# Row fetches of 128 indices, one column group per compare, and 26 dense blocks in the first layer of a three-layer graph network

## The chip, the cores and the metric

The kernel runs on one core of one Trainium2 chip. The metric is the device time of one execution in microseconds, the median of three runs. The chip's engines have short names in the profile: PE (the matrix engine, with PEld for its weight loads), DVE (VectorE), ACT (ScalarE), POOL (GpSimd) and SP (SyncE, which here only issues DMAs). Each runs its own list of instructions in order. GpSimd issues the indirect DMAs that fetch table rows by index.

## The reference, cut to what matters

```python
# x: 6250 x 256 float32; src, dst: 100000 int32, sorted by dst
def gcn(h, W, b):
    h = h @ W
    return segment_sum(h[src] * norm_edge[:, None], dst, n) + b
# src, dst are extended by one loop per node, (i, i)
# deg[d] = number of edges into d (with the loop); norm_edge = deg[src]**-0.5 * deg[dst]**-0.5
h = x                                              # 256
for W, b in ((W1, b1), (W2, b2), (W3, b3)):        # 256 -> 512 -> 512 -> 256
    h = relu(gcn(h, W, b))
out = layernorm(x + h, eps=1e-5)
```

A layer sums, for every node, the rows of the nodes that point to it (16 edges a node on average) and multiplies by a weight matrix. The factors deg**-0.5 belong to the source and the target, so a table holds rows already scaled by the source's factor, and the target's factor comes after the sum.

## The kernel before, in words

**Two ways of summing.** The 6250 nodes are 50 blocks (`NB`) of 125 (`Q`). The sum over incoming edges is made for a whole block at a time, in one of two ways. A *dense* block takes the 125 x 6250 matrix of edge counts (`kept`, stored in bytes) and multiplies it on PE by all rows of the table, held in SBUF as `parts`, a rounded half and a remainder: 50 matmuls at L1467, one for each block of sources, with five blocks' counts converted at a time into a `piece` (L1347). A *gathered* block fetches rows from the table in DRAM with indirect DMAs (L1383) into a ring of row buffers (`rows`). For each block there are 14 *rounds* (`ROUNDS`): round r fetches the source of the r-th edge of each of the 125 nodes, so DVE can add the 125 rows straight to the block's running sum (L1440, `total`). A node with fewer than 14 edges has the index N there, the table's row of zeros. Edges past the 14th are fetched in 128-row lists, three a block (`beyond`), one for two blocks (`pair`) and one for ten (`shared`). ACT and DVE cut these rows into two halves (L1434, L1437), and PE multiplies them by a one-hot matrix (L1399) into the node's place. The index lists are `round_src` (125 partitions), `over_src` and `rest` (128 partitions).

**Which blocks, in which layer.** `layer` (L1267) runs a layer. In layer 1 blocks 0 to 23 (`FEW`) are dense and 26 are gathered: 458 fetches. In layer 2 the first 12 blocks are dense, by `teams` (L1127, matmuls at L1197, three blocks at a time), from the counts kept in layer 1; 38 are gathered: 669 fetches. In layer 3 blocks 0 to 31 (`MANY`) are dense and 18 gathered: 317 fetches. Rows are 256 floats wide in layers 1 and 3 and 512 in layer 2. Layer 2 has 10 row buffers, layer 3 has 19.

**The order of the work.** It is written out by hand. The loop of `layer` takes one fetch at a time (a *chunk*, `now`): it issues fetch `chunk`, adds the round of a few chunks ago (`ADDED`, 3, 5 and 3), cuts and multiplies older lists (`SPLIT`), advances the generators that run beside it (`go_fixed`, `go`), and issues as many dense matmuls as the chunk's number allows:

```python
until = min(len(dense) * NB, begun + int((chunk + 1 - first) * NB / spacing)) if dense else 0
...
if chunk >= total - 1:
    until = len(dense) * NB
```

`spacing` is the number of chunks for each dense block, 16 in layer 1; a dense block also has to wait until its counts are there, and after the last chunk all the remaining matmuls are issued. Each fetch waits until the ring's buffer has been freed by the sum that read it.

**What else runs in layer 1.** The *finder* makes the index lists: `found_rounds` (L576) writes `round_src` for two blocks, with small matmuls into a PSUM bank and a row of small DVE instructions, four of them at L601; `found_beyond` (L615) writes `over_src`. `all_found` runs the first a few pairs ahead of the second. The bank they use (`spot[0]`) is the second half of the PSUM tile whose first half, `near_cols`, holds a copy of `keys`, the numbers of the columns. `counts` (L999) makes the count matrices: for each window of 128 edges it compares edge numbers with column numbers and so has a one-hot matrix of 128 x 125 (`hot_lo`) and one of 128 x 250 (`hot_key`) in bfloat16; PE multiplies the two (L1092), ACT copies the result into the block's counts (L1054), and SP stores them. The compares are made for five windows (`WIDE`) at a time by `compared` (L1018), in three instructions of five, three and two windows, 625, 750 and 500 elements a partition. In layer 1 the counts of blocks 0 to 27 (`FEW + EXTRA`) are made; those of the other four blocks that layer 3 needs are made in layer 2, by `counts_alone`, beside the fetches. `keys` and `slots`, from which `numbers` is cut, lie in SBUF in bfloat16; the copy `near_cols` is float32.

**Between layers.** A block's sum goes through `after1`, `after2` or `after3`: scaling, transposing, matmul with the weights, and the store of the next table. A layer's fetches can begin only when the table before it is complete, so each layer ends in a tail without fetches. `teams` begins its sums when the dense blocks of layer 1 are finished (`while finished < FEW`), and `home` brings back the rows that `teams` had no room for.

Of the kernel before, what the change touches and what calls it, by code (L numbers as in the profile page):

```python
# [13 lines left out]
I32 = mybir.dt.int32  # L14
# [8 lines left out]
P = 128  # L23
# [3 lines left out]
Q = 125  # L27
# [19 lines left out]
FEW = 24  # L47
EXTRA = 4
# [11 lines left out]
ADDS = (False, False, False)  # L60
TURNS = 4
# [338 lines left out]
def sorted_path(ctx: ExitStack, tc: tile.TileContext, x, edges, starts, found, wts, biases, room, late, out):  # L400
# [35 lines left out]
    round_src = const.tile([Q, NE, ROUNDS], I32, name="round_src")  # L436
# [70 lines left out]
    def finder_numbers(spare):  # L507
# [44 lines left out]
        nc.vector.memset(over_lo[:, :, BEYOND], float(P - 1))  # L552
        yield
# [22 lines left out]
    def found_rounds(e):  # L576
# [34 lines left out]
        nc.vector.tensor_single_scalar(round_src[:, e:e + 2], real, float(N), op=ALU.add)  # L611
# [130 lines left out]
    with tc.tile_pool(name="sdeg1", bufs=1) as dp1, tc.tile_pool(name="sdeg", bufs=2) as dp, \  # L742
# [139 lines left out]
        with tc.manual_schedule():  # L882
# [101 lines left out]
    totals = totals_of(one, "sfirst_totals", C, 3) + [first_rows.pop() for _ in range(2 * TURNS - 3)] if ADDS[0] else totals_of(one, "sfirst_totals", C, 3)  # L984
# [14 lines left out]
    def counts(blocks, places, rush=0, at_once=False):  # L999
# [18 lines left out]
        def compared(out, numbers):  # L1018
            shape = list(out.shape)
            nc.vector.tensor_tensor(out, near_cols[:, :shape[2]].unsqueeze(1).to_broadcast(shape),  # L1020
                                    numbers.unsqueeze(2).to_broadcast(shape), op=ALU.is_equal)
# [245 lines left out]
    def layer(i, width, first_b, dense, after, rows, first=0, spacing=None, extras=(), filler=None):  # L1267
# [3 lines left out]
        adds, most_of_acc = ADDS[i], 2 if i == 1 else 3  # L1271
# [7 lines left out]
        together = TURNS if adds else 1  # L1279
        for n in range(0, len(gathered), together):  # L1280
            bs = gathered[n:n + together]
            items += [("round", b, r) for r in range(ROUNDS) for b in bs]
            for b in bs:
                if b == first_b or b % GRP == 0:
                    items.append(("shared", b, b // GRP))
                if b % 2 == 0:
                    items.append(("pair", b, 0))
                items += [("beyond", b, j) for j in range(BEYOND)]
# [65 lines left out]
        def gather(c):  # L1354
# [3 lines left out]
            if kind == "round":  # L1358
                while e not in rounds_ready:
                    next(finding)  # L1360
                if j == 0:
                    sums[b] = totals[b % len(totals)][:Q]
                    by_rows(nc.sync, sums[b], tables[i][b * Q:(b + 1) * Q, :])
                if adds:
                    nc.gpsimd.indirect_dma_start(out=sums[b], out_offset=None, in_=tables[i],
                                                 in_offset=bass.IndirectOffsetOnAxis(ap=round_src[:, e, j:j + 1], axis=0),
                                                 compute_op=ALU.add)
                    return
# [21 lines left out]
        def kind_at(c):  # L1390
            return items[c][0] if 0 <= c < total else None
# [32 lines left out]
        with tc.manual_schedule():  # L1424
            for chunk in range(total + lag):
# [12 lines left out]
                if kind_at(chunk - ADDED[i]) == "round" and not adds:  # L1438
# [258 lines left out]
    layer(0, C, FEW, few, after1, first_rows, 16, 16.0,  # L1697
# [28 lines left out]
    totals = totals_of(ctx, "slate_totals", C, 2 * TURNS if ADDS[2] else 3)  # L1726
# [184 lines left out]
```

## Time and profile before

| | |
|---|---|
| median of three runs | 2670.28 us (2648.01 to 2673.69) |
| profiled execution, its own time | 2664.05 us |
| its span in the trace | 2662.3 us |
| busy: PE, DVE, POOL, ACT | 1923.2 (72%), 1781.3 (67%), 1804.2 (68%), 1099.5 us (41%) |
| moved by DMA | 452.97 MB, 170 GB/s over the span |
| of it in GpSimd's queue (row fetches) | 274.22 MB, 217984 packets |
| row fetches | 1148 by `round_src`, 287 by `over_src`, 9 by `rest` |
| chain that ended last | DMA 49%, DVE 22%, PE 10%, issue 10% |

In the profile, a group of instructions has its line, engine, operation, output and inputs by the program's names, the shapes as partitions x elements, the number of instructions, the busy time and the mean of one in ns, and then the idle time of the engine ahead of them with what ended it (`<-DVE total L1440` means that a DVE instruction of L1440 released it). A line of the time line has the start in us, the duration, and in brackets the idle time before it. A stretch has, for each engine, busy us and the number of instructions, then the granted clock of the matrix engine (1.00 is full), the busy share of the 16 DMA engines and what they moved. A fetch's DMA view shows a window in 40 slices, with the busy share of the DMA engines in tenths in each.

### The profile page before, as it was taken

To read this page: it belongs to the slowest core of one execution; us is meant where nothing else is said; L and a number is where in the kernel's file an instruction comes from. 1 tells how busy PE (TensorE), PEld (TensorE's weight loads), DVE (VectorE), ACT (ScalarE), POOL (GpSimd) and SP (SyncE) were. 2 spreads that over 40 slices of the span, in tenths; PEclk is the share of its full clock that TensorE was granted. 3 is DMA by queue.
4 is the path that set the end of the run, shared out by engine and by line. 5 is a ranking of instruction groups with operands and counts; after the bars stand their busy time and mean duration, and the time that the engine had idled before them with its cause. 6 is when DMAs were issued, how large, how long until landed. Compare 5 with 4: busy or idle time off the path is not lost.

```text
span 2662.3 us, 29214 instructions
## 1 busy us (share of the span) xinstructions
PE 1923.2 (72%) x7865; PEld 1410.1 (53%) x7865; DVE 1781.3 (67%) x3890; ACT 1099.5 (41%) x2136; POOL 1804.2 (68%) x1487
## 2 busy tenths in 40 slices
PE   3367777777788765778767777777674579898885
PEld 2245555555565443556545655555453357676663
DVE  5789889897898835656566565556665536666656
ACT  1455556555676632333334333332331234343432
POOL 2365656665677746777777677667778858787776
PEclk9988888898999776788887888788887779999998
DMA  6434434343455689999999999999997747776764
GB/s 141 121 92 113 116 91 132 110 110 110 116 145 142 187 193 206 204 207 230 224 211 222 221 223 217 207 224 216 211 216 196 190 127 169 169 174 168 172 169 116
DMA packets 331628, 452.97 MB, mean 170 GB/s; under 512 B 169007, under 2 KB 219174, under 8 KB 331453
## 3 DMA queue, kind: packets, MB, share of 16 engines
q0 software_dynamic: 217984, 274.22, 46.4%
q1 hardware_dynamic: 97629, 164.94, 25.3%
q10 hardware_dynamic: 15840, 11.86, 1.9%
q8 instruction: 63, 1.03, 0.2%
q14 instruction: 112, 0.92, 0.1%
HBM read 392.59 MB, written 57.00 MB: 169 GB/s over the span
## 4 chain that ended last, share of the span: by engine, by line
DMA 49%; DVE 22%; PE 10%; issue 10%; POOL 5%; ACT 2%; SPq 1%; ACTq 0%; DVEq 0%; POOLq 0%
DMA room<-tab,round_src 36%; DMA room<-tab,over_src 9%; DVE room L1020 6%; DVE total L1440 5%; POOL room L1383 5%; PE sacc L1467 1%; DMA room<-in_x 1%; DVE halves L1437 1%; DMA total<-tab 1%; PE mat_ps L1467 1%; DMA room<-tab,rest 1%; DVE st L1521 1%; ACT halves L1434 1%; DVE emask L601 1%; PE smm L1467 1%
## 5 line engine op out<-in xcount | busy, mean ns | idle before, releaser
L1383 POOL DMA_INDIRECT room<-tab,round_src x1148 | 1481.2, 1290 | 626.9 <-DVE total L1440 238.6
L1440 DVE TENSOR_TENSOR total<-total,room 125x256 f32<-125x256 f32 (+1 forms) x1148 | 625.8, 545 | 584.8 <-DMA room<-tab,round_src 565.5
L1383 POOL DMA_INDIRECT room<-tab,over_src x287 | 291.6, 1016 | 144.4 <-issue 41.4
L1347 ACT CAST piece<-room 125x625 fp32r<-125x625 uint8 x457 | 321.4, 719 | 123.7 <-PE win_ps L1467 30.2
L1434 ACT CAST halves<-room 128x256 fp32r<-128x256 f32 (+1 forms) x296 | 149.3, 508 | 528.1 <-DMA room<-tab,over_src 480.0
L1020 DVE TENSOR_TENSOR room<-near_cols,slots 128x625 bf16<-128x625 f32 (+2 forms) x420 | 325.2, 803 | 52.6 <-PE near_cols L625 26.3
L1197 PE MATMUL sacc<-parts 125*125 125x512 f32 x400 | 183.1, 510 | 188.2 <-DVE parts L1161 167.2
L1399 PE MATMUL sacc<-halves,shot 128*125 128x512 f32 x525 | 206.1, 492 | 108.3 <-ACT halves L1434 63.0
L1467 PE MATMUL win_ps<-parts,piece 125*125 125x512 f32 x750 | 214.7, 430 | 19.1 <-DVE piece L1347 10.2
L1437 DVE TENSOR_TENSOR halves<-room,halves 128x256 fp32r<-128x256 f32 (+1 forms) x296 | 159.1, 544 | 101.2 <-ACT halves L1434 100.5
L1467 PE MATMUL smm<-parts,piece 125*125 125x512 f32 x755 | 210.2, 419 | 19.0 <-DVE piece L1347 17.2
L1197 PEld LDWEIGHTS sacc<-parts 125*125 125x125 f32 x400 | 85.6, 219 | 245.9 <-DVE parts L1161 206.4
L1399 PEld LDWEIGHTS sacc<-halves,shot 128*125 128x125 f32 x525 | 115.6, 226 | 177.4 <-ACT halves L1434 76.0
L1467 PE MATMUL mat_ps<-parts,piece 125*125 125x512 f32 x700 | 190.7, 413 | 10.2 <-DVE piece L1347 8.9
L1092 PEld LDWEIGHTS <-room 128*125 128x125 bf16 x700 | 101.6, 155 | 164.1 <-issue 117.3
L1467 PEld LDWEIGHTS win_ps<-parts,piece 125*125 125x125 f32 x750 | 144.6, 201 | 57.2 <-DVE piece L1347 12.3
L1467 PEld LDWEIGHTS smm<-parts,piece 125*125 125x125 f32 x755 | 138.1, 192 | 58.5 <-issue 17.9
L1197 PE MATMUL mat_ps<-parts 125*125 125x512 f32 x400 | 160.2, 487 | 2.2 <-DVE room L1561 2.2
L1467 PE MATMUL sacc<-parts,piece 125*125 125x512 f32 x450 | 160.4, 471 | 0.0
L1159 ACT CAST parts<-parts 125x512 fp32r<-125x512 f32 x200 | 122.4, 617 | 87.0 <-PE smm L1197 45.1
L1197 PE MATMUL smm<-parts 125*125 125x512 f32 x400 | 156.2, 476 | 0.1
L1467 PEld LDWEIGHTS mat_ps<-parts,piece 125*125 125x125 f32 x700 | 127.9, 191 | 44.1 <-DVE piece L1347 11.6
(401 smaller groups left out, 3226.0 us busy)
## 6 DMA issues: line engine op xcount, KB each, us to landing
parts<-tab SPq DMA_DIRECT2D x104, 448.0 KB
kept<-room SPq DMA_DIRECT2D x32, 683.6 KB
room<-kept SPq DMA_DIRECT2D x32, 683.6 KB
room<-tab,round_src POOLq DMA_INDIRECT x1148, 6.6
tab<-st SPq DMA_DIRECT2D x62, 224.0 KB
total<-tab SPq DMA_DIRECT2D x38, 224.0 KB
parts<-kept SPq DMA_DIRECT2D x60, 136.7 KB
room<-in_x SPq DMA_DIRECT2D x50, 112.0 KB
```

Source lines behind the costliest of these rows:

```text
L601: nc.vector.tensor_single_scalar(mask, off, float(by_n - KF), op=ALU.is_ge)
L1020: nc.vector.tensor_tensor(out, near_cols[:, :shape[2]].unsqueeze(1).to_broadcast(shape), numbers.unsqueeze(2).to_broadcast(shape), op=ALU. ...
L1092: nc.tensor.matmul(bank[:Q, len(pair) * 256:][:, :G * NB], lhsT=hot_lo, rhs=hot_key, start=True, stop=True)
L1159: nc.scalar.copy(to[:, :HID], row)
L1197: nc.tensor.matmul(team_banks[n][:Q], lhsT=team_pieces[(g * CUTS + k // PIECE) % 2][n][:, k % PIECE, :], rhs=both_parts[u % 3][:, h * HID: ...
L1347: convert(piece, made_or_read[:, c * PIECE:(c + 1) * PIECE, :])
L1383: nc.gpsimd.indirect_dma_start(out=row, out_offset=None, in_=tables[i], in_offset=bass.IndirectOffsetOnAxis(ap=at, axis=0))
L1399: nc.tensor.matmul(acc[:Q, :size], lhsT=hots[b][:, k], rhs=two[:, c0:c0 + size], start=(k == c0 == 0), stop=(k == BEYOND + 1 and c0 + size ...
L1434: nc.scalar.copy(two[:, :width], landed[chunk - hi_lag])
L1437: nc.vector.tensor_sub(two[:, width:], landed.pop(chunk - lo_lag), two[:, :width].bitcast(F32))
L1440: nc.vector.tensor_add(own, own, landed.pop(chunk - ADDED[i])[:Q])
L1467: nc.tensor.matmul(acc_d[:Q], lhsT=got[done // PIECE][:, k % PIECE, :], rhs=parts[:, k], start=(k == 0), stop=(k == NB - 1))
```

## The change

It has three parts.

1. **Rounds with 128 indices.** `round_src` gets 128 partitions; partitions 96 and up are first set to N, the row of zeros, and the finder then writes the first 125. A round's fetch now has 128 indices and fills all 128 rows of its buffer. The sum still reads 125.
2. **One column group an instruction.** `compared` loops over the windows; each window is one tensor_scalar with the column numbers from `keys` in SBUF as its tensor and the window's number, one bfloat16 scalar per partition, as its operand. Five windows are ten instructions, of 125 and 250 elements, where there were three.
3. **26 dense blocks in layer 1.** `FEW` is 26 instead of 24, `EXTRA` 0 instead of 4. Layer 1 has 24 gathered blocks, 423 fetches; layer 1 makes 26 counts instead of 28, layer 2 six instead of four. A dense block's matmuls come 15 chunks apart instead of 16.

A path that was switched off (`ADDS`, sums made by the DMA) is removed with its constant `TURNS`; by it the finder's rounds run one pair ahead of the other lists instead of two, and the first layer's fetches wait for one pair fewer.

```diff
-FEW = 24
-EXTRA = 4
+FEW = 26
+EXTRA = 0
...
-ADDS = (False, False, False)
-TURNS = 4
...
-    round_src = const.tile([Q, NE, ROUNDS], I32, name="round_src")
+    round_src = const.tile([P, NE, ROUNDS], I32, name="round_src")
...
+        nc.vector.memset(round_src[96:], N)
...
-        nc.vector.tensor_single_scalar(round_src[:, e:e + 2], real, float(N), op=ALU.add)
+        nc.vector.tensor_single_scalar(round_src[:Q, e:e + 2], real, float(N), op=ALU.add)
...
-        ahead = TURNS // 2
+        ahead = 1
...
-            while FEW - FIRST_EDGES + TURNS - 1 not in rounds_ready:
+            while FEW - FIRST_EDGES + 1 not in rounds_ready:
...
         def compared(out, numbers):
-            shape = list(out.shape)
-            nc.vector.tensor_tensor(out, near_cols[:, :shape[2]].unsqueeze(1).to_broadcast(shape),
-                                    numbers.unsqueeze(2).to_broadcast(shape), op=ALU.is_equal)
+            for w in range(out.shape[1]):
+                nc.vector.tensor_scalar(out[:, w], keys[:, :out.shape[2]], numbers[:, w:w + 1], None, op0=ALU.is_equal)
...
-                row, at = row[:Q], round_src[:, e, j:j + 1]
+                at = round_src[:, e, j:j + 1]
...
-    layer(0, C, FEW, few, after1, first_rows, 16, 16.0,
+    layer(0, C, FEW, few, after1, first_rows, 16, 15.0,
```

More of the change, by code (lines that the diff above doesn't have):

```diff
@@ L1270, in layer @@
         gathered = every[first_b:]
-        adds, most_of_acc = ADDS[i], 2 if i == 1 else 3
+        most_of_acc = 2 if i == 1 else 3
         going = []
@@ L1278, in layer @@
         items = []
[L1279 to L1288, printed above, removed]
+        for b in gathered:
+            items += [("round", b, r) for r in range(ROUNDS)]
+            if b == first_b or b % GRP == 0:
+                items.append(("shared", b, b // GRP))
+            if b % 2 == 0:
+                items.append(("pair", b, 0))
+            items += [("beyond", b, j) for j in range(BEYOND)]
         total = len(items)
```

11 lines of the change are left out of this document (3 added, 8 removed).

## The prediction

> **What bounds the kernel now.** I read the page first, then busy time by stretch (cut where the fetches of one layer begin and end), then the groups and the time line of the engine that set the pace in each stretch, and last the DMA view of single fetches. The page's span and its two groups of row fetches:
>
> ```profile
> span 2662.3 us, 29214 instructions
> ...
> L1383 POOL DMA_INDIRECT room<-tab,round_src x1148 | 1481.2, 1290 | 626.9 <-DVE total L1440 238.6
> ...
> L1383 POOL DMA_INDIRECT room<-tab,over_src x287 | 291.6, 1016 | 144.4 <-issue 41.4
> ```
>
> 1148 round fetches, one list index per node of a block (125), cost GpSimd 1290 ns on average. The 287 fetches of over_src, with 128 indices into rows of the same width, cost 1016. Busy time by stretch; columns are PE, weight load, DVE, ACT, POOL, granted clock, DMA share, GB/s:
>
> ```profile
> core 0: us, PE busy (x) PEld busy (x) DVE busy (x) ACT busy (x) POOL busy (x), PEclk, DMA share, GB/s
> 0.00:105.00 105.00, 38.70 (x229) 29.24 (x229) 62.67 (x233) 34.14 (x110) 15.09 (x37) 1.00 0.60 146
> 105.00:730.00 625.00, 450.71 (x2148) 317.73 (x2149) 538.79 (x1420) 345.77 (x693) 383.64 (x322) 0.89 0.39 108
> 730.00:945.00 215.00, 172.23 (x719) 117.65 (x717) 179.74 (x346) 140.94 (x267) 170.16 (x142) 0.90 0.60 163
> 945.00:970.00 25.00, 22.04 (x75) 15.98 (x76) 11.46 (x21) 11.95 (x22) 0.00 (x0) 0.80 0.53 136
> 970.00:2144.00 1174.00, 810.38 (x2952) 603.15 (x2950) 688.83 (x1067) 377.83 (x695) 850.17 (x669) 0.81 1.01 213
> 2144.00:2167.00 23.00, 20.95 (x99) 16.50 (x99) 5.28 (x10) 10.40 (x20) 0.05 (x1) 0.87 0.22 69
> 2167.00:2649.00 482.00, 405.34 (x1641) 308.44 (x1640) 290.24 (x786) 177.23 (x329) 385.03 (x317) 0.95 0.68 166
> 2649.00:2663.00 14.00, 2.86 (x5) 1.39 (x5) 4.26 (x11) 1.25 (x4) 0.00 (x0) 0.50 0.08 24
> ...
> 2143.00:2146.00 3.00, 0.00 (x0) 0.00 (x0) 1.38 (x2) 0.62 (x1) 0.94 (x1) 0.56 0.77 249
> ```
>
> Four regimes stand here. Layer 1 up to 730 us (316 of its 458 fetches; six of the 322 are others) has DVE busy 538.79 of 625, 86%. Layer 1 from 730 to 945 (142 fetches), after the finder has ended, has GpSimd at 170.16 of 215. Layer 2 (669 fetches, 1174 us, 1.755 each) has a DMA share of 1.01. Layer 3 (317 fetches, 482 us, 1.52 each) has GpSimd at 385.03 and PE at 405.34. Between them lie tails without fetches of 25, 23 and 14 us.
>
> How much of a stretch GpSimd really fills needs the gap between two fetches, and the group in layer 2 says what a round fetch costs there. The last two lines are landing times, of 970 to 2144 us and of 105 to 730:
>
> ```profile
> 1499.61 1.21 POOL L1383 DMA_INDIRECT room<-tab,round_src  x1 [0.30 <-issue]
> 1501.13 1.21 POOL L1383 DMA_INDIRECT room<-tab,round_src  x1 [0.31 <-issue]
> ...
> L1383 POOL DMA_INDIRECT room<-tab,round_src x532: 1205/1220/1738, 970.3 to 2138.5; - x178
> L1383 POOL DMA_INDIRECT room<-tab,over_src x133: 941/959/1651, 998.6 to 2143.1; - x133
> ...
> L1383 POOL DMA_INDIRECT room<-tab,round_src x532 | 706.5, 1328 | 276.9 <-DVE total L1440 127.4 <-issue 71.0 <-DMA parts<-kept 25.6
> ...
> DMA to landing us min/median/max: 4.0/11.5/18.7
> ...
> DMA to landing us min/median/max: 2.7/4.1/7.1
> ```
>
> Even where it waits for nothing, a fetch follows the last by 0.305 us. So GpSimd fills 385.03 + 317 x 0.305 = 482 of 482 us in layer 3 and 170.16 + 142 x 0.305 = 213 of 215 in late layer 1: it is the bound there. In layer 2 it fills 850.17 + 204 = 1054 of 1174; the rest are waits for the sum that frees a row buffer, behind landings of 11.5 us where layer 1 has 4.1. There the DMA is the bound.
>
> **The change, part by part.**
>
> *Round fetches with 128 indices.* The fastest round fetch takes 1205 ns, the fastest of 128 indices 941, medians 1220 and 959: I take 0.26 us off each, for it is the same line of code, the same kind of instruction and the same tables, and only the number of indices differs. What it does to the transfers, two fetches each alone on the DMA show; the first is a round fetch (window 711 to 714.4, slices of 85 ns), the second has 128 indices (317.2 to 319, slices of 45 ns):
>
> ```profile
> DMA  0000000012973004012103233331300000000000
> ...
> DMA packets 128, 0.13 MB, mean 38 GB/s; under 512 B 93, under 2 KB 98, under 8 KB 128
> ...
> DMA  0000098994980266822000000000000000000000
> ...
> DMA packets 48, 0.13 MB, mean 73 GB/s; under 512 B 16, under 2 KB 16, under 8 KB 48
> ```
>
> The round fetch moves its rows in 30 large packets and 5 of one row, plus 93 tiny ones, and after the burst of tiny ones keeps about three tenths of the engines busy. That fits five engines with 25 rows each (six packets of four rows and one single). The 128-index fetch has 32 large packets, 16 tiny ones and about nine tenths of the engines. So the change spreads each round fetch over all engines and drops some 77 tiny packets; it adds 3 rows, 2.4%.
>
> [...]
>
> *Layer 2.* GpSimd's floor becomes 850.17 - 532 x 0.26 + 669 x 0.305 = 916 us, 1.37 a fetch. The DMA has 1174 us x 213 GB/s = 250 MB to move and 3.3 MB more for three rows in each round fetch. At today's rate that is 1189 us, the upper bound. The row 2143 to 2146, where the last three fetches of the layer, all of 128 indices, drain with the ends of some round fetches, moves 249 GB/s at a share of 0.77, 323 at a full one; layer 2 gets 213 from a share of 1.01. At 323 the 253 MB need 785 us, under GpSimd's floor. I take that row, being the nearest to what the layer will consist of, so the bound passes from DMA to GpSimd: 950 us (1.42 a fetch), the floor and 34 us for what the streams of counts still collide with. PE then stands at 810 of 950 and DVE at 700, both below the floor. The two more blocks of counts there add 10 groups of compares, 18 us of DVE under these 950. The tail stays 23.
>
> *Layer 3.* GpSimd: 385.03 - 252 x 0.26 + 317 x 0.305 = 416 us. PE comes close behind with 405 busy, so I take neither alone but 434 (1.37 a fetch), between 416 and 463 (half the saving). Its tail stays 14.
>
> *Compares.* A group of five windows was three instructions with two tensors, from PSUM; it becomes ten with one tensor and one scalar, from SBUF: five of 125 and five of 250 elements. The DVE starts an instruction before the last one's record ends, so a price is the distance of starts:
>
> ```profile
> 249.45 1.66 DVE L1020 TENSOR_TENSOR room<-near_cols,slots 128x625 bf16<-128x625 f32 x2
> 251.02 0.42 DVE L1440 TENSOR_TENSOR total<-total,room 125x256 f32<-125x256 f32 x1
> ...
> 251.74 0.67 DVE L1020 TENSOR_TENSOR room<-near_cols,slots 128x500 bf16<-128x500 f32 x1
> 252.32 0.41 DVE L1440 TENSOR_TENSOR total<-total,room 125x256 f32<-125x256 f32 x1
> ...
> 31.79 0.28 DVE L522 TENSOR_SCALAR elater<-elanes,w 128x125 bf16<-128x125 f32 x1
> 31.99 0.28 DVE L523 TENSOR_SCALAR esince<-elanes,w 128x125 bf16<-128x125 f32 x1
> 32.18 0.14 DVE L526 TENSOR_SCALAR w<-w 128x1 f32<-128x1 f32 x1
> 32.24 0.14 DVE L527 TENSOR_SCALAR w<-w 128x1 f32<-128x1 f32 x1
> ...
> 38.66 0.20 DVE L823 TENSOR_SCALAR near<-near 128x160 bf16<-128x160 bf16 x1
> 38.77 1.46 DVE L826 TENSOR_TENSOR sfull<-scols,sdlo 128x1260 bf16<-128x1260 f32 x1
> ```
>
> Before: 251.02 - 249.45 and 252.32 - 251.74, 2.15 us a group. An instruction on one element takes 0.06. With 160 two-byte elements and a constant it takes 0.11, so 0.05 for the elements, 0.31 ns each; with 125 four-byte ones and a scalar read per partition 0.20, of which I put 0.06 to the scalar and 0.08 to the elements, 0.64 ns each. The new form is two bytes in and out, with a scalar per partition: 0.12 + 125 x 0.31 ns = 0.16 and 0.12 + 250 x 0.31 ns = 0.20, 1.80 a group. With 0.64 ns it is 2.40. The slow end is 1 ns an element, as the two-tensor form has (2.15 us for 1875 elements, three times 0.06 taken off): 0.245 and 0.37, 3.08 a group. I take 1.80, from the row whose types are the same. What else the compares meet, from the groups and one line of 105 to 730 us (the x8 line is of 0 to 105):
>
> ```profile
> L1020 DVE TENSOR_TENSOR room<-near_cols,slots 128x625 bf16<-128x625 f32 x98 | 79.0, 806 | 32.3 <-PE near_cols L625 18.9 <-PE near_cols L638 6.8 <-PE near_cols L589 4.4
> L1020 DVE TENSOR_TENSOR room<-near_cols,slots 128x500 bf16<-128x500 f32 x97 | 65.5, 676 | 15.2 <-PE near_cols L625 7.4 <-PE near_cols L638 5.1 <-PE near_cols L581 0.7
> ...
> L601 DVE TENSOR_SCALAR emask<-eoff 125x2 int32<-125x2 f32 x8 | 1.3, 168 | 0.2
> ...
> L601 DVE TENSOR_SCALAR emask<-eoff 125x2 int32<-125x2 f32 x68 | 17.8, 262 | 1.8
> ...
> 256.08 0.53 DVE L601 TENSOR_SCALAR emask<-eoff 125x2 int32<-125x2 f32 x1
> ```
>
> The compares now wait 32.3 + 15.2 us for the finder's matmuls, because they read the bank in which those write; the new ones read keys in SBUF and don't. Half of it I count as gained (24 us); the other half I leave to the next wait, since the finder's own instructions still stand in the DVE's order. Against it: a tensor_scalar of two elements takes 168 ns before the first fetch and 262 beside fetches, up to 0.53. So a fetch holds such an instruction up by as much as 0.36 us, and the old compares, means of 806 and 676 with no such spread, were not of that kind. If a third of the 316 fetches meets a compare, that is 38 us; shorter fetches should hold less, so I put 25, between 0 and 92 (0.094 on each of 980 instructions).
>
> [...]
>
> *Layer 1.* Up to 730 us: 625 - 98 x 0.35 - 24 + 25 = 592 for the same 316 fetches. Then 458 - 35 - 316 = 107 fetches (two blocks fewer are gathered): GpSimd's floor falls from 1.50 to 1.50 - 0.26 x 112/142 = 1.30, DVE stands at 179.74/142 = 1.27 less 0.1 for compares plus 0.1 for holds; two engines that close give 1.40 each, 150 us. Then the tail. In the built program's order on PE, 91 dense matmuls stand behind the last fetch, since the counts of block 26 are ready only there; at the 0.25 us that layer 3 shows (405.34/1641) they take 23 us with nothing to fetch, and the last blocks' own chains about 22, where 25 are spent now: 45.
>
> *Start.* One pair of blocks fewer is found before the first fetch: 105 becomes 102.
>
> **Sum.** 102 + 592 + 150 + 45 + 950 + 23 + 434 + 14 = 2310. The profiled execution took 2664.05 us with a span of 2662.3, so 2312 is my time. The runs shown have a median of 2670.28, 0.2% over that execution. A change of about 1% is what a measurement of this kernel can tell from none.
>
> **Rivals.**
>
> *A, the DMA stays the bound of layer 2.* For it: no whole stretch of the table moves over 213 GB/s, and rows of 2 KB at random places may be what limits it. Against: the row 2143 to 2146. Then layer 2 takes 1189 and the total is 2312 + 239 = 2551.
>
> *B, the compares run at one element a cycle or so* (3.08 a group). For it: column groups of 125 elements are odd and start at odd places. Against: L522 has 125 too. 625 + 98 x 0.93 - 24 = 692 up to 730 us, then DVE at 1.27 + 0.3 x 0.93 = 1.54, some 1.65 a fetch, 177: 2312 + 100 + 27 = 2439. With A as well it is about 2680, no change.
>
> *C, slower: the zero row is a hot spot.* Each round fetch would end with three reads of one row, all in the last engine's share. Layer 1 has 336 round fetches then, 1120 in all; the other 289 take some 376 us, starts and tails 184, so the total passes 2664 when that engine needs 1.9 us a round fetch; at 2.1 it is 2912. Against: spare rounds of nodes with few edges read that row already, about a quarter of the nodes in the last round at 16 edges a node, and no round fetch of layer 2 takes over 1738 ns on GpSimd or 18.7 us to land.
>
> *D, the price does not go by the count.* Then GpSimd keeps 1054 in layer 2 (1070 with collisions), 482 in layer 3 and 1.51 in late layer 1 (162): 102 + 592 + 162 + 45 + 1070 + 23 + 482 + 14 = 2490, 2492 as a time. Nothing in the rows but their different lists speaks for it.
>
> **Chances.** The forecast 0.70, A 0.12 (0.02 of it with B), B alone 0.10, D 0.05, C 0.03. The likeliest alone spans 2200 (every floor met: 557 and 139 in layer 1, 916, 416) to 2420. The range goes to 2500, which takes in B and D and leaves out A and C. Faster by over 1%: 0.95; within 1%: 0.02 (A with B); slower: 0.03.
>
> **What would show it.** Right: round fetches at a median near 960 ns in every stretch; a landing time in layer 2 near 6 us and more than 250 GB/s; layer 3 with GpSimd at its floor and PE over 90%; compares 0.16 and 0.20 apart; a stretch of some 45 us at the end of layer 1 in which PE alone is busy. Wrong: round fetches still at 1.2 us (D), 213 GB/s in layer 2 with a share of 1.0 (A), compares 0.25 and 0.37 apart or DVE over 95% in layer 1 (B).

## The result, and the profile after

The changed kernel took 2503.2 us (median of four runs, 2496.86 to 2517.89) against 2661.04 for the kernel before (2648.01 to 2673.69): a ratio of 0.9415, 95% interval 0.9343 to 0.9487. It is faster, by 158 us; the forecast was 349, and 2503 lies just above the top of its range. The profiled execution took 2497.86 us. Its busy time by stretch, in the stretches of the prediction (the first is cut at 660 us here, while fetch 316 comes at 673; columns are PE, weight load, DVE, ACT, POOL, granted clock, DMA share, GB/s):

```profile
core 0 of [0], span 2495.4 us
...
0.00:102.00 102.00, 37.78 (x229) 29.16 (x229) 58.97 (x233) 32.82 (x110) 15.12 (x37) 1.00 0.61 144
102.00:660.00 558.00, 424.80 (x2080) 296.52 (x2078) 487.52 (x2061) 332.77 (x667) 323.20 (x313) 0.92 0.40 119
660.00:850.00 190.00, 155.31 (x662) 108.27 (x663) 134.96 (x528) 123.96 (x236) 118.27 (x116) 0.89 0.45 135
850.00:896.00 46.00, 41.11 (x159) 28.86 (x158) 12.59 (x26) 27.43 (x48) 0.00 (x0) 0.96 0.41 112
896.00:1957.00 1061.00, 771.94 (x3074) 585.63 (x3073) 698.24 (x1323) 399.83 (x735) 716.94 (x669) 0.85 0.86 244
1957.00:1982.00 25.00, 22.74 (x113) 18.32 (x112) 4.95 (x9) 11.42 (x24) 0.00 (x0) 0.93 0.20 52
1982.00:2472.00 490.00, 415.22 (x1632) 315.01 (x1632) 278.94 (x760) 175.50 (x326) 312.03 (x317) 0.92 0.62 163
2472.00:2496.00 24.00, 5.64 (x19) 3.68 (x17) 14.17 (x38) 1.90 (x6) 0.00 (x0) 0.64 0.10 29
```

Layer 1 and its tail came out near the sum (743 us from the first fetch, at 105.9, and 47; forecast 742 and 45), but by luck: the part up to fetch 316 was 25 us shorter than forecast and the rest 26 longer. Layer 2 took 1061 (forecast 950) and layer 3 took 490 (forecast 434, 482 before). Yet nothing in layer 3 is full: GpSimd is busy 312 of 490 us, PE 415, and the DMA share is 0.62. A round fetch costs GpSimd what was forecast, here in layer 2:

```profile
L1373 POOL DMA_INDIRECT room<-tab,round_src x532: 945/949/4902, 897.6 to 1950.9; - x178
```

So GpSimd has its work cheaper, and something else holds it up: with the gaps of 0.305 us it fills 312 + 97 = 409 of the 490 us of layer 3. The time line of layer 3 shows what. These are all lines of PE, DVE and ACT in 18 us, without the weight loads:

```profile
2009.36 0.49 DVE L1342 CAST piece<-room 125x625 fp32r<-125x625 uint8 x1 [7.82 <-PE mat_ps L1457]
2009.77 1.79 DVE L1430 TENSOR_TENSOR total<-total,room 125x256 f32<-125x256 f32 x4
2009.90 1.43 PE L1457 MATMUL mat_ps<-parts,piece 125*125 125x512 f32 x5 [1.18 <-issue]
2022.75 0.71 ACT L1342 CAST piece<-room 125x625 fp32r<-125x625 uint8 x1 [17.60 <-remote]
2023.52 2.50 PE L1457 MATMUL mat_ps<-parts,piece 125*125 125x512 f32 x5 [12.19 <-ACT piece L1342]
2027.67 1.95 ACT L1342 CAST piece<-room 125x625 fp32r<-125x625 uint8 x3 [4.20 <-remote]
2027.75 0.49 DVE L1342 CAST piece<-room 125x625 fp32r<-125x625 uint8 x1 [16.20 <-remote]
```

"remote" means that no instruction of the program ends at the time of the release. PE ends five matmuls at 2011.3 and has no next piece. ACT converts that piece only at 2022.75. It waits for PE's semaphore alone: the pieces lie in six buffers in turn (`slate_pieces`), so a conversion waits for the matmuls that read the piece six before. In the record these end at 2004.08 (the second of the two matmuls in the first line below); ACT starts 18.7 us later, 0.07 after the record of a signal of PE at 2022.68. In a later run of the same kernel (e4, below) the same conversion starts 0.09 us after those matmuls:

```profile
2003.45 0.63 PE L1457 MATMUL win_ps<-parts,piece 125*125 125x512 f32 x2
...
1800.35 1.10 PE L1457 MATMUL win_ps<-parts,piece 125*125 125x512 f32 x4
...
1801.54 0.72 ACT L1342 CAST piece<-room 125x625 fp32r<-125x625 uint8 x1 [1.61 <-PE win_ps L1457]
```

DVE stands still with such a conversion too, and the sums behind it in its order, which free the row buffers, come late: the next one starts at 2028.87, and only then can GpSimd fetch again. In the whole of layer 3 GpSimd waits 69.9 us for these sums (third line; us in total, times, longest us), in e4 21.0 (fourth line):

```profile
2028.87 0.42 DVE L1430 TENSOR_TENSOR total<-total,room 125x256 f32<-125x256 f32 x1
...
2029.56 0.94 POOL L1373 DMA_INDIRECT room<-tab,round_src  x1 [5.90 <-DVE total L1430]
...
POOL room L1373 <- DVE total L1430: 69.9, 46, 5.9
...
POOL room L1373 <- DVE total L1430: 21.0, 69, 0.3
```

The longest rows with "remote" in the waits of the whole trace; the first two are of layer 2, the others of layer 3:

```profile
ACT room L1601 <- remote: 98.1, 11, 16.2
ACT parts L1157 <- remote: 97.6, 13, 13.5
...
DVE piece L1342 <- remote: 85.0, 12, 16.2
...
ACT piece L1342 <- remote: 77.1, 18, 17.6
```

The trace of before has no such row. Two counts over the whole trace go with it. It holds 18,382 records of semaphore updates where the trace of before, with about as many signals, holds 47,053; the gaps begin at about 110 us, soon after the first row fetch. And some 170 times PE's next recorded signals come in a burst with no signalling matmul that ends within 0.3 us of them; counted from the first signalling matmul behind the previous record, about 740 us in all. Both figures move with the way the 0.3 us are taken (147 to 188 times, 643 to 779 us), and the sum is an upper bound of the lateness, since a lost record looks the same. In the trace of before both are 0. That trace comes from an execution of its own (2664.05 us, not among the four above), and no record says on which chip it was taken.

### The profile page after: what moved, and what is told of

Its sections match the earlier page's. It is cut to its first block, busy times and chain, and to the rows that moved or that the text cites. A ratio compares the mean times of both kernels' runs of the same rounds, so it can differ in the third digit from the quotient of the medians.

```text
span 2495.4 us, 30287 instructions
## 1 busy us (share of the span) xinstructions
PE 1874.5 (75%) x7955; PEld 1385.5 (56%) x7955; DVE 1690.3 (68%) x4972; ACT 1105.6 (44%) x2149; POOL 1485.6 (60%) x1452
## 4 chain that ended last, share of the span: by engine, by line
PE 15%; issue 12%; POOL 6%; DVE 6%; another core or an unknown queue 5%; DMA 5%; ACT 2%; ACTq 0%; DVEq 0%; SPq 0%; POOLq 0%
POOL room L1373 6%; PE win_ps L1457 3%; PE mat_ps L1457 3%; PE smm L1457 3%; DMA room<-tab,round_src 3%; DVE total L1430 2%; PE sacc L1389 2%; DMA room<-tab,over_src 1%; ACT piece L1342 1%; PE win_ps L1590 1%; DVE halves L1427 1%; PE sacc L1195 0%; PE mat_ps L1195 0%; DMA total<-tab 0%
## 5 line engine op out<-in xcount | busy, mean ns | idle before, releaser
L1373 POOL DMA_INDIRECT room<-tab,round_src x1120 | 1165.7, 1041 | 713.4 <-issue 276.6
L1019 DVE TENSOR_SCALAR room<-keys,slots 128x125 bf16<-128x125 bf16 (+1 forms) x1300 | 263.4, 287 | 31.7 <-remote 14.3
L1457 PE MATMUL win_ps<-parts,piece 125*125 125x512 f32 x900 | 260.3, 430 | 19.8 <-issue 12.4
L1159 DVE TENSOR_TENSOR parts<-parts 125x512 fp32r<-125x512 f32 x200 | 137.4, 687 | 134.6 <-ACT parts L1157 100.4
L1389 PE MATMUL sacc<-halves,shot 128*125 128x512 f32 x515 | 181.0, 445 | 57.7 <-issue 24.0
L1195 PE MATMUL sacc<-parts 125*125 125x512 f32 x400 | 161.1, 470 | 79.0 <-issue 33.4
L1457 PEld LDWEIGHTS win_ps<-parts,piece 125*125 125x125 f32 x900 | 170.8, 199 | 67.9 <-issue 21.0
L1590 PE MATMUL win_ps<-room,w_sb 128*128 128x250 f32 x640 | 165.3, 404 | 30.0 <-DVE st L1623 12.9
L1590 PEld LDWEIGHTS win_ps<-room,w_sb 128*128 128x128 f32 x640 | 130.3, 207 | 56.6 <-issue 19.0
L1342 DVE CAST piece<-room 125x625 fp32r<-125x625 uint8 x94 | 47.1, 501 | 166.3 <-remote 85.0
```

The source lines that it names most:

```text
L1019: nc.vector.tensor_scalar(out[:, w], keys[:, :out.shape[2]], numbers[:, w:w + 1], None, op0=ALU.is_equal)
L1159: nc.vector.tensor_sub(to[:, HID:], row, to[:, :HID].bitcast(F32))
L1195: nc.tensor.matmul(team_banks[n][:Q], lhsT=team_pieces[(g * CUTS + k // PIECE) % 2][n][:, k % PIECE, :], rhs=both_parts[u % 3][:, h * HID: ...
L1342: convert(piece, made_or_read[:, c * PIECE:(c + 1) * PIECE, :])
L1373: nc.gpsimd.indirect_dma_start(out=row, out_offset=None, in_=tables[i], in_offset=bass.IndirectOffsetOnAxis(ap=at, axis=0))
L1389: nc.tensor.matmul(acc[:Q, :size], lhsT=hots[b][:, k], rhs=two[:, c0:c0 + size], start=(k == c0 == 0), stop=(k == BEYOND + 1 and c0 + size ...
```

## The experiments

### Is it the kernel? (e4, e5, e11, e13, e15, e18)

The changed kernel, unaltered, was run again.

> The changed kernel once more, on the chip that runs the three others. Theory L: late signals and missing update records again, layers 1060 and 489 within 10, 2503 within 15. If they were an accident of one chip or one execution, they are gone here, and the time with them (about 2400 or lower).

> The changed kernel a third time. On record it took 2503 us with late matrix-engine signals in its trace, in e4 2208 without. Theory S (the record's slowness belongs to that session, not to the kernel): 2208 within 10 and no late signals, whatever chip it is. Theory K (the kernel itself has two states): in one of these executions the 2500 comes back.

> The changed kernel a fourth time, as the yardstick for e9 and e10 on the same chip. Theory S: 2208 within 10, no late signals. Theory K: 2500 with late signals.

It took 2208.4, 2206.1 and 2206.9 us on three chips, ratios to the kernel before on the same chip of 0.8331 (0.829 to 0.8372), 0.8296 (0.8263 to 0.833) and 0.8308 (0.8281 to 0.8334). There are no "remote" waits and 46,888 semaphore records in e4. Of the conversions of layer 3 that had to wait, the median one starts 0.09 us after the matmuls that free its buffer; in the record it is 4.1 us (1.2 in the trace of before). The stretches of e4:

```profile
0.00:101.00 101.00, 37.01 (x227) 28.68 (x228) 58.24 (x231) 32.04 (x110) 15.10 (x37) 1.00 0.60 145
101.00:620.00 519.00, 410.14 (x2067) 289.22 (x2066) 485.26 (x2057) 332.44 (x664) 321.55 (x312) 0.94 0.43 127
620.00:781.00 161.00, 151.26 (x695) 106.65 (x694) 140.02 (x541) 127.80 (x247) 120.23 (x118) 0.98 0.55 165
781.00:823.00 42.00, 37.82 (x141) 26.65 (x140) 8.97 (x17) 23.79 (x41) 0.00 (x0) 0.92 0.40 111
823.00:1754.00 931.00, 758.77 (x3088) 577.82 (x3086) 703.27 (x1323) 402.37 (x739) 719.47 (x669) 0.90 0.98 278
1754.00:1779.00 25.00, 21.00 (x95) 16.48 (x96) 4.26 (x8) 10.30 (x20) 0.00 (x0) 0.80 0.18 49
1779.00:2194.00 415.00, 388.79 (x1647) 305.05 (x1645) 289.10 (x787) 178.81 (x330) 316.84 (x317) 0.98 0.72 193
2194.00:2207.00 13.00, 2.87 (x5) 1.11 (x4) 3.92 (x10) 1.03 (x3) 0.00 (x0) 0.50 0.09 26
```

GpSimd now fills layer 2 (719 + 669 x 0.305 = 923 of 931) and layer 3 (317 + 97 = 414 of 415). Against the record, layer 1 is 68 us shorter, layer 2 130, layer 3 75, the end 11. Then it was run on three more chips.

> The changed kernel once more, if it may be on another chip than the three before. Theory S (what made the record slow belongs to that session): 2208 within 10, every matrix-engine signal recorded and timely. Theory K (a state of the kernel that any chip can fall into): 2500, late signals and most semaphore records missing, as in the record.

> The changed kernel, to tell which kind of chip runs e14: 2208 without late signals, or about 2480 to 2500 with them.

> The changed kernel, to tell which kind of chip runs e16 and e17: 2208 without late signals, or 2460 to 2500 with them.

It took 2473.9 (0.9313, 0.9275 to 0.9351), 2460.5 and 2493.7 us (two runs, one and one), with the record's marks each time: about 18,300 to 19,100 semaphore records, "remote" waits, a median conversion in layer 3 of 3.8 to 4.0 us after its matmuls, layer 2 at 1037 to 1052 and layer 3 at 481 to 491. The kernel before takes the same on both kinds, medians of 2654 to 2656 on the first and 2658 to 2668 on the second. So theory S falls: it isn't one session. Theory K as e13 states it forecast these times, but no sitting showed both levels. All runs of one sitting agreed, and each chip was met in one sitting, so a kind of chip and a kind of sitting can't be told apart; below I say the first kind (2207) and the second (2460 to 2503), and "kind of chip" stands for both.

### The parts, on the first kind (e1, e2, e6, e7)

e1 is the kernel before with 128-index rounds alone:

```diff
-    round_src = const.tile([Q, NE, ROUNDS], I32, name="round_src")
+    round_src = const.tile([P, NE, ROUNDS], I32, name="round_src")
...
+        nc.vector.memset(round_src[96:], N)
...
-        nc.vector.tensor_single_scalar(round_src[:, e:e + 2], real, float(N), op=ALU.add)
+        nc.vector.tensor_single_scalar(round_src[:Q, e:e + 2], real, float(N), op=ALU.add)
...
-                row, at = row[:Q], round_src[:, e, j:j + 1]
+                at = round_src[:, e, j:j + 1]
```

> The kernel before with one part of the change alone: round fetches have 128 indices, the last three the zero row. In the profile after, layer 2 took 1060 us (1175 before) and layer 3 489 (483 before), and matrix-engine signals (semaphore updates that other engines wait for) came several microseconds late, 741 us of lateness in 169 bursts, where before had none. Theory L (late signals come with the 128-index rounds and take back most of their gain): late signals appear here too, layer 2 about 1060, layer 3 about 490, total about 2520. Theory M (matmul bound: with shorter fetches the matrix engine itself is the limit of layer 3, and of part of layer 2): the same layer times, but the lateness has no part in them; told apart by whether layer 3 keeps its 490 where lateness is absent. If the other two parts carry the gain instead, the total is above 2600.

2295.0 us, 0.8664 (0.862 to 0.8707). No late signals; layer 1 went from 845 to 808 (from here on it is counted from GpSimd's first wait for a fetch, 4 to 6 us ahead of the first fetch), layer 2 from 1175 to 907, layer 3 from 483 to 415. Both of my theories had taken the record's layers for granted and missed.

e2 is the changed kernel with 125 indices a round:

```diff
-                at = round_src[:, e, j:j + 1]
+                row, at = row[:Q], round_src[:Q, e, j:j + 1]
```

> The changed kernel with its round fetches back at 125 indices, all else as changed. Theory L: no late signals, layer 2 about 1175, layer 3 about 483, both bound as before; layer 1 about 810 instead of 845 (fewer fetches, cheaper compares, tail 25 longer); total about 2660 - 10 = 2650. If layer 3 or layer 2 is slower or faster than in the kernel before by over 10 us, the other parts reach further than layer 1, against the prediction's sum.

2562.6 us, 0.9649 (0.9599 to 0.9699), 354 above e4. Layer 1 took 709, 100 us less than I had expected of the other two parts; layer 2 1209, 33 more than before, with six blocks' counts there; layer 3 483. The profiled execution was the longest of the four, 20 us over their median, and in e17, the same kernel, layer 2 took 1190; so part of the 33 may be the execution. The gains of e1 and e2, 361 and 93 us, add up to 454; all three parts together brought 447 on this chip (e4).

e6 is the changed kernel with the old compares:

```diff
-            for w in range(out.shape[1]):
-                nc.vector.tensor_scalar(out[:, w], keys[:, :out.shape[2]], numbers[:, w:w + 1], None, op0=ALU.is_equal)
+            shape = list(out.shape)
+            nc.vector.tensor_tensor(out, near_cols[:, :shape[2]].unsqueeze(1).to_broadcast(shape),
+                                    numbers.unsqueeze(2).to_broadcast(shape), op=ALU.is_equal)
```

> The changed kernel with the old compares (three two-tensor instructions a group, reading the PSUM bank), all else as changed. In e4 98 groups of compares took 178 us of DVE against 212 in the kernel before, and the DVE's idle time up to fetch 316 fell from 86 to 37. Theory C (only the price counts, 0.34 us a group, 130 groups in layer 1): 2208 + 35 to 44 = about 2250. Theory W (the wait for the finder's bank goes with it): another 25 to 50, 2275 to 2295.

2259.9 us, 54 over e5 on its chip. Layer 1 is 742 instead of 678, but layer 2 is 919 instead of 937. Up to fetch 316 the time is 594 us instead of e4's 531: 211 us of compares instead of 178, idle DVE 64 instead of 37, and 4 more in the rest. So the wait goes with the compares, as theory W has it for layer 1; layer 2 gives 18 us back, and the total lies nearer to theory C's 2250.

e7 undoes the blocks: FEW 24, EXTRA 4, spacing 16.

> The changed kernel with 24 dense blocks in layer 1, counts of 28 there and spacing 16, as before; 128-index rounds and new compares stay. By e4's rows: 35 fetches more at 1.32 in late layer 1 (+46), two blocks' counts more in layer 1 (10 groups of 1.84 and their sums, +20 to 25), a tail of 23 in place of 42 (-19), layer 2 907 in place of 930 (-23, two blocks' counts fewer): 2208 + 25 to 30 = 2235. Rival (the dense burst at the end of layer 1 and the counts in layer 2 cost more than the blocks save): 2208 or less.

2218.7 us, 13 over e5: layer 1 726 (+48), its tail 22 (-19), layer 2 917 (-20). I had expected 2235, or 2208 and less by the rival; it lies between. The two extra dense blocks bring little: of the 48 us of layer 1 they give back 19 in the tail, where their last matmuls stand behind the last fetch, and 20 in layer 2, where two more blocks' counts are made.

### The zero row and the price of a fetch (e3, e8)

e3 lets the three extra indices of a round point at different ordinary rows:

```diff
-        nc.vector.memset(round_src[96:], N)
+        nc.gpsimd.iota(round_src[96:], pattern=[[ROUNDS, NE], [1, ROUNDS]], base=0, channel_multiplier=150)
```

> The changed kernel with the three extra indices of each round pointing at different ordinary rows in place of the one zero row (the sums don't read these three rows, so the output is that of the reference). Theory Z (the zero row is a hot spot: its repeated reads are what keeps layer 2 at 1060 and layer 3 at 489): layer 2 about 950, layer 3 about 434, total about 2340. Theories L and M: no change, 2503 within 10.

2207.2 us beside 2208.4 on the same chip: the zero row costs nothing. Rival C is refuted.

e8 varies the count:

```diff
-                at = round_src[:, e, j:j + 1]
+                n = (120, 126, 112)[i]
+                row, at = row[:n], round_src[:n, e, j:j + 1]
...
-                    nc.vector.tensor_add(own, own, landed.pop(chunk - ADDED[i])[:Q])
+                    n = (120, 125, 112)[i]
+                    nc.vector.tensor_add(own[:n], own[:n], landed.pop(chunk - ADDED[i])[:n])
```

> The changed kernel with round fetches of 120 indices in layer 1, 126 in layer 2 and 112 in layer 3 (in layers 1 and 3 the sums then leave out the last 5 and 13 nodes of each block; the other work is as it was). It measures what sets a round fetch's price on GpSimd, 1.21 us with 125 and 0.945 with 128. [...] Theory F (only the full 128 partitions are fast): all three near 1.2. [...]

One run, 2315.7 us. The round fetches of layers 1, 2 and 3 (fastest, median, slowest in ns):

```profile
L1374 POOL DMA_INDIRECT room<-tab,round_src x336: 978/987/3330, 105.1 to 772.8; - x168
L1374 POOL DMA_INDIRECT room<-tab,round_src x532: 992/1007/4052, 820.7 to 1853.2; - x178
L1374 POOL DMA_INDIRECT room<-tab,round_src x252: 929/936/1563, 1884.5 to 2295.6; - x126
```

Layer 2 by stretch:

```profile
820.00:1859.00 1039.00, 788.58 (x3083) 593.05 (x3081) 706.30 (x1322) 404.09 (x739) 756.68 (x669) 0.86 1.02 247
```

120 indices cost 987 ns, 126 cost 1007, 112 cost 936, 128 cost 949 in the record (967 in layer 2 of e4) and 125 cost 1214 in the kernel before. Only 125 stands out, so theory F falls. What in the count sets the price, five counts don't settle, and no run here shows how a fetch of 120, 126 or 112 is spread over the DMA engines. Layer 2 with 126 took 1039 us where e4, with 128, has 930: the DMA was full again, at a share of 1.02 and 247 GB/s, where e4 moves 278 at 0.98.

### What bounds layer 2 now, and a faster version (e12, e9, e10)

e12 loads half of each table row for the sums of three blocks in layer 2:

```diff
-                by_rows(nc.sync, streamed[p % RING], tables[1][k * Q:(k + 2) * Q, :].rearrange(...))
+                by_rows(nc.sync, streamed[p % RING][:, :, :HID // 2], tables[1][k * Q:(k + 2) * Q, :HID // 2].rearrange(...))
```

> The changed kernel with the table rows for the three-block sums of layer 2 loaded by half their columns (224 KB in place of 448 in each of 100 loads; the other half of the sums is then made from old data). 22 MB fewer of the 253 of layer 2, where the DMA share was 0.98 and GpSimd 924 of 931 us. Theory G (GpSimd is the limit and the DMA follows): layer 2 stays at 920 to 931, the share falls to about 0.9. Theory D (the DMA, being full, draws out the fetches on GpSimd): round fetches fall from a mean of 1076 toward 1000 ns and layer 2 to about 880.

One run, 2202.2 us. Layer 2 of e12, and its group of round fetches:

```profile
817.00:1751.00 934.00, 760.38 (x3086) 584.51 (x3084) 701.84 (x1323) 403.13 (x739) 729.10 (x669) 0.89 0.86 250
...
L1373 POOL DMA_INDIRECT room<-tab,round_src x532 | 582.6, 1095 | 202.9 <-issue 92.2 <-DMA parts<-kept 40.9 <-DMA room<-tab,round_src 28.6
```

And of e11 on the same chip:

```profile
818.00:1754.00 936.00, 760.76 (x3085) 577.78 (x3083) 703.02 (x1322) 402.30 (x739) 720.49 (x669) 0.90 0.98 276
```

The DMA share fell to 0.86, layer 2 did not get shorter (934 beside 936), and the mean fetch did not get cheaper (1095 ns beside 1076 in e11, shown below): GpSimd is the bound (theory G), with the DMA close behind in the kernel as changed.

e9 uses the new compares in layer 1 only:

```diff
         def compared(out, numbers):
+            if not at_once:
+                shape = list(out.shape)
+                nc.vector.tensor_tensor(out, near_cols[:, :shape[2]].unsqueeze(1).to_broadcast(shape),
+                                        numbers.unsqueeze(2).to_broadcast(shape), op=ALU.is_equal)
+                return
             for w in range(out.shape[1]):
```

> The changed kernel with the new compares in layer 1 only; the counts made in layer 2 use the old two-tensor compares. In layer 2 GpSimd is the limit after the change (719 busy + 204 in gaps of 931 us), and a round fetch there averaged 1076 ns beside new compares (e4) and 1036 beside old ones (e6); layer 2 took 930 and 919. Theory H (the one-scalar compares hold up GpSimd's fetches, a cost where GpSimd is the limit): layer 2 about 919, total 2208 - 11 = 2197. Rival (e6's 11 us came from its later start or another order): 930 and 2208.

2194.1 us (2189.53 to 2200.54) beside 2206.9 for e11 on its chip (2205.92 to 2210.12), 0.826 of before (0.8229 to 0.8291): faster than both kernels, the changed one by 13 us, and their ranges don't meet. The group of round fetches in layer 2, in e9:

```profile
L1378 POOL DMA_INDIRECT room<-tab,round_src x532 | 555.3, 1044 | 212.3 <-issue 99.9 <-DMA parts<-kept 42.7 <-DMA room<-tab,round_src 23.2
```

And in e11:

```profile
L1373 POOL DMA_INDIRECT room<-tab,round_src x532 | 572.3, 1076 | 214.1 <-issue 105.9 <-DMA parts<-kept 44.1 <-DMA room<-tab,round_src 19.0
```

Theory H holds: the one-scalar compares draw out GpSimd's fetches by 17 us in all, and layer 2 was 16 shorter without them.

e10 adds FEW 24 and EXTRA 2 to e9.

> As e9, and 24 dense blocks in layer 1 with counts of 26 made there: no dense burst behind the last fetch. From e7 (layer 1 726 with counts of 28, tail 22): two blocks' counts fewer, 10 groups of 1.84 and their sums, make 706; layer 2 919: total 102 + 706 + 22 + 919 + 24 + 414 + 14 = 2201. Rival (GpSimd sets late layer 1 and fewer counts gain nothing there): 726 and 2220.

2208.9 us, 0.8299 (0.8264 to 0.8333): layer 1 724, its tail 17. It is 15 us slower than e9. Layer 1 came out as the rival had it (726); its total of 2220 was 11 too high.

### What sets the late signals off (e14, e16, e17, on chips of the second kind)

> The kernel of e8 once more (round fetches of 120, 126 and 112 indices in layers 1, 2 and 3; sums leave out the last nodes' rounds in layers 1 and 3). On a chip of the e4, e5, e11 kind: 677, 1039, 417 us, as in e8. [...]

e14 is e8's kernel, in one run; e15 says the chip was of the second kind. Layers 1, 2 and 3 took 732, 1052 and 483 us where e8 had 677, 1039 and 417, with "remote" waits in all three. So 120, 126 and 112 indices have them too: it doesn't take 128. All four counts have cheaper fetches than 125 (936 to 1007 ns in e8 and the record, 1214 in the kernel before), so the next runs vary the pace.

e16 puts a pause behind each round fetch:

```diff
+    pause = const.tile([1, 100], F32, name="pause")
...
+            if kind == "round":
+                nc.gpsimd.memset(pause, 0.0)
+                nc.gpsimd.memset(pause, 0.0)
```

> The changed kernel with two small memsets on GpSimd behind every round fetch (a private tile, no one reads it), so that its round fetches follow each other about as slowly as those of 125 indices do (1.5 us in place of 1.25), with their 128 indices kept. On a chip of e4's kind: layer 3 about 480, GpSimd being its limit, layer 2 about 1000, no late signals. On a chip of the record's, e13's and e15's kind, theory V (fetches that follow too closely bring the late signals): layer 3 again about 480, but every signal recorded and timely. Theory X (the wide fetch itself brings them, at any rate): late signals again, layer 3 above 500.

> The kernel of e2 (round fetches of 125 indices, all else as changed). On either kind of chip, by theories V and X: 2560 within 20, layer 3 about 483, no late signals, all semaphore records there. If late signals come here too, on the second kind of chip, the round fetches are not what sets them off.

One run each. The pause was longer than meant, 1.89 us from fetch to fetch, so e16's 2822.5 us is mostly pause. It has no "remote" waits, and its bursts of PE signals without a matmul fell from some 170 (720 us, e18 on the same chip) to 13 (some 36 us). Some records are still missing (38,517 are there). e17 took 2568.6, e2's time, with 40 to 70 bursts (50 to 100 us), one "remote" row (5.7 us), and 31,853 records; in layer 3 its median conversion starts 1.3 us after its matmuls, as in e2 on the first kind. The 31,853 are a miss for both theories, which had all records there. Layer 3 of e16:

```profile
2229.00:2806.00 577.00, 441.94 (x1644) 333.13 (x1642) 297.33 (x787) 177.87 (x329) 404.27 (x821) 0.87 0.51 139
```

And of e17:

```profile
2070.00:2553.00 483.00, 405.48 (x1642) 308.51 (x1641) 292.53 (x786) 176.44 (x328) 385.63 (x317) 0.95 0.67 165
```

With 128 indices kept and the pace cut, the lateness all but went, which speaks for theory V (close succession) and against X. It isn't clean: e17's layer 1 has some lateness at 125, and the pause of e16 slows the whole kernel. So a limit on all signals of the core together (layer 3, with the same fetches and dense blocks, takes 415 us in e4 and 482 in the kernel before) isn't told from one on fetches in close succession. Open stays what in those chips or sittings makes records go missing and PE's signals come late. Both appear together in the record, but e17 lost a third of its records with hardly a signal late. Whether the lateness would be there without the recording can't be told, for every run here was recorded.

## Why the prediction was right and wrong

| stretch, us | forecast | record | e4 |
|---|---|---|---|
| start | 102 | 106 | 106 |
| layer 1, to fetch 316 | 592 | 567 | 531 |
| layer 1, the rest | 150 | 176 | 144 |
| its tail | 45 | 47 | 43 |
| layer 2 | 950 | 1060 | 930 |
| its tail | 23 | 26 | 25 |
| layer 3 | 434 | 489 | 414 |
| end | 14 | 24 | 14 |
| sum | 2310 | 2495 | 2207 |

**Against the record** the terms that failed are those of layer 2 (950, measured 1060) and layer 3 (434, measured 489): 165 of the 185 us by which the sum was too short. Both start from GpSimd's floor and add to it only collisions and PE's work. The step that failed is the one under both: that a wait ends when the work behind it ends. In the record GpSimd, with its gaps, fills 921 of 1061 us in layer 2 and 409 of 490 in layer 3; the other 140 and 81 us it waits, where e4 has 8 and 1. Signals of PE arrive late, 18.7 us after the matmul in the case shown, and no rival had that: every one of them let an engine or the DMA become the bound. The trace of before shows no late signal, and the prediction took its releases, all prompt, for a property of the machine. Rival D's 2492 lies near the record by luck, for its mechanism, a fetch price that stays, is refuted by the 949 ns.

Layer 3 is where this is cleanest: 75 us above e4, with every engine less than 85% busy. PE's granted clock is lower there too (0.92 against 0.98) and its busy time 26 us longer, but PE isn't full, so the clock alone doesn't make the 75 us. That the change brings some 158 to 197 us on one kind of chip and 447 to 449 on the other is shown; the cause of the lateness isn't.

**On the first kind** the sum was 103 us too long, and the terms can be judged. The 2207 us lie at the low end of the likeliest span; by the floors that the prediction names there, that end is 2212 and not 2200, and its 557 us for the first part of layer 1 are not worked out.

- *Start.* One pair fewer found did not shorten it: the 3 us were wrong. Before (first line) and in the record (second), as in e4, the first fetch waits for DVE's copies of the table, not for the lists:

```profile
105.41 3.55 POOL L1383 DMA_INDIRECT room<-tab,round_src  x1 [23.41 <-DVE parts L880]
...
105.88 3.31 POOL L1373 DMA_INDIRECT room<-tab,round_src  x1 [21.34 <-DVE parts L879]
```

- *Round fetch.* 0.26 us off was right to 0.01 (949 in place of 1214). The reason given, that only the number of indices differs, fell short: 126 cost 1007 and 112 cost 936 (e8). Rival D is refuted.
- *Layer 2.* The bound passed from DMA to GpSimd as forecast (floor 916; GpSimd fills 923 of 931; e12). But the row 2143 to 2146, scaled to 323 GB/s, had promised a DMA with room to spare; it is at a share of 0.98 with 278. So rival A's bound was close: with 126 indices (e8) the DMA sets the layer again, at 1039 us, though not at A's 1189. The 34 us for collisions were 14.
- *Layer 3.* 414 against a floor of 416: PE at 389 of 415 cost nothing, and the 18 us allowed for it were wrong. In e4 it has a granted clock of 0.98. (The upper bound of 463 was not half the saving, either; that is 449.)
- *Compares.* Up to fetch 316, 98 groups took 178 us of DVE in place of 212, by the distances of their starts, 1.82 each: 33 us gained, 34 forecast. Rival B is refuted. The compares lost about 2 us to fetches where I had put 25; the price fell on GpSimd's side (a round fetch in layer 2 at a mean of 1076 ns in e11 and 1044 in e9, 17 us in all). By what means the one lengthens the other no run here shows.
- *The bank wait.* I let half of it go; the DVE's idle time fell by 49 us (86 to 37), not 24. Its other instructions took 12 us less beside shorter fetches (the finder's copies, L602 before, 13.8 in place of 17.9), which I had at nothing. With the holds, these are the 61 us by which the first term was too long: 25 + 12 + about 24.
- *Tails.* 45 forecast, 43 measured: the dense burst is there, and with the counts in layer 2 it eats most of what two dense blocks save (e7: 13 us net).

## What to carry to other kernels

Measure an indirect DMA at a few index counts before settling on one: going from 125 to 128, with three wasted rows, took a fetch from 1214 to 949 ns here and brought 361 us alone, on the first kind of chip. Where GpSimd's fetches are the bound, try the compares without one-scalar DVE instructions, which here lengthened a fetch from 1044 to 1076 ns (e9, e11); where the DVE is the bound, try them, for up to fetch 316 they took 178 us of it in place of 211 (e4, e6). And when a trace after shows idle engines that wait for each other, with releasers that no instruction explains, run the same program again, on another chip and at another time, before you explain it.

## What the runs showed of the hardware

One program, unaltered, took 2206 to 2208 us on three chips and 2460 to 2503 on others, each steady within 1% where it ran more than once, while the kernel before took 2654 to 2668 beside all of them. In the traces of the record, e13, e15 and e18, of 2460 to 2503 us, PE's signals reached ACT and DVE late (18.7 us after the matmul in the case shown of the record; a median of 3.8 to 4.1 us for the conversions of layer 3 that waited, 0.09 in e4), and there were 18,300 to 19,100 semaphore records where e4 has 46,888.

The median price of a round fetch on GpSimd isn't monotonic in its indices: 936 ns for 112, 987 for 120 and 1007 for 126 (e8), 1214 for 125 (the kernel before) and 949 for 128 (the record).
